# Attention block with group norm: one range test of the softmax sums per pair of heads, bias additions at the head of a burst, and a weight test that takes its minimum one chain later

## The chip, the cores and the metric

The kernel runs on one core of a Trainium2 chip. The metric is the device time of one execution in microseconds (us). Before the change the median of three timed runs was 1619.6 us (1618.7 to 1620.19). A separate execution was profiled; all durations below come from its trace.

## The reference

The input is `x` with 4 images of 512 channels and 48 x 48 = 2304 positions. Group norm (32 groups of 16 channels) is followed by a projection to queries, keys and values of 8 heads with 64 channels each, rounded to half precision; then softmax attention over the 2304 positions, an output projection in single precision, and the residual.

```python
hn = _group_norm(x, gn_scale, gn_bias)
qkv = jnp.einsum('oc,bchw->bohw', qkv_w, hn) + qkv_b[None, :, None, None]
qkv = qkv.reshape(b, 3, num_heads, d, t).astype(jnp.float16)
q, k, v = (qkv[:, 0], qkv[:, 1], qkv[:, 2])
scale = jnp.asarray(1.0 / math.sqrt(math.sqrt(d)), dtype=jnp.float16)
w = jnp.einsum('bhct,bhcs->bhts', q * scale, k * scale)
w = jax.nn.softmax(w, axis=-1)
a = jnp.einsum('bhts,bhcs->bhct', w, v).astype(jnp.float32)
out = jnp.einsum('oc,bchw->bohw', proj_w, a.reshape(b, c, hh, ww)) + proj_b[None, :, None, None]
return x + out
```

## The kernel before

**Two paths.** `fast_path` computes softmax without subtracting a maximum. While it runs it collects tests: every sum of exponentials must lie between `SUM_MIN` = 256 and `SUM_MAX` = 60000, and the split of the output weights into two parts must be exact. At the end the tests are added up into a flag; only where one failed does `general_path` compute everything again. With these inputs the fast path's result stands.

**Units of work.** Two heads are handled together, so there are 16 pairs `g` (4 per image `b`). For each pair the 2304 query positions are cut into five blocks `j`, four of 512 and one of 256 (`QBLOCKS`, `NQ` = 5). A block is worked off in bursts of three score tiles of 128 x 1024: `scores` issues the matmuls on TensorE (PE, L1084) and the exponentials on ScalarE (ACT, L1091); `add` sums the tiles on VectorE (DVE, L1140 and L1145); `values`, two bursts behind, multiplies with the values (PE, L1109). When a block ends, `avx` copies the product out of PSUM (DVE, L1118), `add_up` sums the accumulated exponentials over the partitions (PE, `sl`, L1168), `rows` copies the result (`slx`, L1184) and has the sync engine's queue (SP) send it as two small DMAs into a tile `sums` of 128 x 8. Then `check_sums` tests that tile on GpSimd (POOL, L1206 and L1207: twice a comparison and a product into `fine`), `invert` takes reciprocals, `spread` sends them back over a DRAM row into `ib`, and `divide` multiplies on POOL (`att`, L1233).

**Beside the bursts** stands a list `beside` of other PE work: the chains of the query and key projections for later pairs (`pqk`, L813, evacuated on DVE at L824), those of the values (`pv`, L865) and of the output projection of the image before (`pr`, L971). Each burst calls `fill(n)` once, which issues pieces of the list by a credit: the estimated work up to its due time over the bursts left. All chains beside the bursts share one PSUM bank (`ps_w`, one buffer), so a chain can start only when the one before has been evacuated by DVE; `av` and `sl` also share one bank (`ps_av`).

**The output weights** are loaded in four pieces (`wproj`, SP) and split during the first pair, a piece after each pair of `q` and `k` chains: on DVE the high part `whi` (L574), the remainder (L575) and its half precision form `wlo` (L578); on POOL the difference (L579) and its comparison with zero (L580); then on DVE the minimum over the comparison (L581, `tests<-wproj`).

**The output projection** of image `b - 1` runs during the next image, that of the last image in its own last pair and the tail. `att32` converts two of the four products of a block on POOL (`a`, L961) and two on ACT; `residual` loads `x` again (`r`, L916) and notes in `unbiased` that the bias must be added two bursts later. `add_bias` does so on POOL (L927); `proj_run` forces it for the rows it needs. DVE then adds the projection to `r` (L995), SP stores it.

**What sets the order.** The program is written by hand in the loop over bursts `n`: every engine works off its own queue in exactly this order, and waits on the others by semaphores. Within a burst the order is: loads due, `scores`, `rows` of a block that ended, `add`, (with an ended block) `fill`, `values`, `check_sums` and `invert`, `spread`, `divide`, (otherwise) `fill`, the joins, and then the biases that are due. `idle_once` puts a number of empty instructions into the queues of the first bursts.

Of the kernel before, what the change touches and what calls it, by code (L numbers as in the profile page):

```python
# [12 lines left out]
F32 = mybir.dt.float32  # L13
# [462 lines left out]
def fast_path(  # L476
# [93 lines left out]
        nc.sync.dma_start(wproj[c], proj_wT[bass.ts(c, P), :])  # L570

    def split_wproj(c):
        w = wproj.pop(c)
        nc.vector.tensor_scalar(whi[:, c, :], w, UP, None, ALU.mult)  # L574
        nc.vector.scalar_tensor_tensor(  # L575
            w, w, UP, whi[:, c, :].bitcast(F32), ALU.mult, ALU.subtract
        )
        nc.vector.tensor_copy(wlo[:, c, :], w)  # L578
        nc.gpsimd.tensor_tensor(w, w, wlo[:, c, :], ALU.subtract)  # L579
        nc.gpsimd.tensor_scalar(w, w, 0.0, None, ALU.is_equal)  # L580
        nc.vector.tensor_reduce(split_ok[:, c : c + 1], w, AX.X, ALU.min)  # L581

    mhalf = const.tile([P, 2], F32, name="mhalf")
    nc.gpsimd.memset(mhalf, -0.5)
# [15 lines left out]
            channel_multiplier=sign,  # L600
        )

    tests = const.tile([P, 2 * QB // P + NC], F32, name="tests")
    nc.gpsimd.memset(tests, 1.0)
    fine, split_ok = tests[:, : 2 * QB // P], tests[:, 2 * QB // P :]

# [439 lines left out]
    def expect_end(*engines):  # L1048

        taken = nc.values_load(  # L1050
            nothing[0:1, 0:1],
            engines=engines,
            min_val=0,
            max_val=1,
            skip_runtime_bounds_check_because="it is a constant",
        )
        tc.mark_branch_hint_location("fallback", taken, engines)
# [122 lines left out]
    def rows(g, j, sl):  # L1180

        o, n = QBLOCKS[j]
        sx = work.tile([P, QB], F32, tag="rows", name=f"slx_{g}_{j}")
        nc.vector.tensor_copy(sx[:, :n], sl[:, :n])  # L1184
        sm = small.tile([P, 2, QB // P], F32, tag="sums", name=f"sums_{g}_{j}")
        for h in range(2):
            nc.sync.dma_start(sm[:, h, : n // P], sx[h * D : h * D + 1, :n])
        sums[g, j] = sm
        return sx
# [7 lines left out]
        )  # L1197

    def check_sums(g, j):
        n = QBLOCKS[j][1]  # L1200
        sm = sums[g, j][:, :, : n // P]
        ok = fine.rearrange("p (h i) -> p h i", h=2)[:, :, : n // P]
        for op, limit in ((ALU.is_ge, SUM_MIN), (ALU.is_le, SUM_MAX)):
            t = small.tile([P, 2, QB // P], F32, tag="in", name=f"in_{g}_{j}")
            t = t[:, :, : n // P]
            nc.gpsimd.tensor_scalar(t, sm, limit, None, op)  # L1206
            nc.gpsimd.tensor_tensor(ok, ok, t, ALU.mult)  # L1207

    def invert(g, j):
        n = QBLOCKS[j][1]  # L1210
# [37 lines left out]
    def put_run(run, *args, when=None, after=0):  # L1248

        put([piece(0.05, lambda: run(*args), when=when)], after)  # L1250
# [41 lines left out]
    def put_qk(g, part, blocks=range(NQ)):  # L1292

        for j in blocks:
            put(qk_chain(g, part, j), (g - 2) * per_pair - 1, g)
# [39 lines left out]
    for b in range(B):  # L1335
        g = b * NPAIR
        old = b - 1
        if b == 0:
            for j in range(NQ):
                if j < NC:  # L1340
                    put_run(load_wproj, j)
                if j > 0:
                    put_run(split_wproj, j - 1)
                put_qk(g + 1, 1, (j,))
                put_qk(g + 1, 0, (j,))
            for block in SPARE:
                put_run(reload, *block)
# [183 lines left out]
    for n in range(end):  # L1531
        now[0] = n
        idle_once("sync", "scalar", "gpsimd")
        summed = block_at(n - BEHIND - 1)
        if not summed:
            load_due(n)
        wanted(stream[n][0])
        inside = n - BEHIND == soon[1]
        scores(stream[n], (lambda: values(stream[n - BEHIND])) if inside else None)
        if summed:  # L1540

            rows(*summed, add_up(*summed))
            load_due(n)
        if inside:
            expect_end(kinds.DVE)
        if n > 0:
            add(stream[n - 1])
        filled = summed or n - BEHIND - 1 in soon
        if filled:

            fill(n)
        if n >= BEHIND and not inside:
            values(stream[n - BEHIND])
        if block_at(n - BEHIND - 2):
            check_sums(*block_at(n - BEHIND - 2))
            invert(*block_at(n - BEHIND - 2))
        if block_at(n - BEHIND - 3):
            spread(*block_at(n - BEHIND - 3))
        if block_at(n - BEHIND - 4):

            divide(*block_at(n - BEHIND - 4))
        if not filled:
            fill(n)
        while joins:
            joins.popleft()()
        while unbiased and unbiased[0][0] <= n:
            add_bias()
        if n - BEHIND in soon:
            g, j = stream[n - BEHIND][:2]
            sx = rows(g, j, add_up(g, j))  # L1570
            if n - BEHIND == soon[1]:
                divide_here(g, j, sx, avx[g, j], nc.gpsimd)
        if n - BEHIND - 1 == soon[0]:
            check_sums(g, j)
            invert(g, j)
        if n - BEHIND - 2 == soon[0]:
            spread(g, j)
            divide(g, j)
# [143 lines left out]
```

## Time and profile before

| | |
|---|---|
| median of three runs | 1619.6 us |
| profiled execution: time, span | 1622.01 us, 1620.3 us |
| TensorE clock granted, mean | 0.994 |
| DVE busy | 1151.4 us (71%) |
| ACT busy | 1269.6 us (78%) |
| POOL busy | 453.4 us (28%), in 551 instructions |
| tests on POOL (L1206, L1207) | 100.2 and 62.9 us, 158 instructions each |
| bias additions on POOL (L927) | 108.2 us, 80 instructions |
| weight test on DVE (L581) | 2.7 us, 4 instructions |

The span runs from the first to the last instruction; the execution's own time is 1.7 us longer. Busy times are sums over one engine. In the views by stretches (windows) a row gives the busy time of every engine, the number of its instructions, and the mean of the clock that TensorE was granted; a stretch in which PE is busy less than its length is one in which PE waited. In the views of waits a row reads: engine, instruction and line, "<-" the engine and line that released it, then total us, number, longest. In timelines a row is start, duration, engine, line, operation, and in brackets the idle time before it with its releaser; instructions of one kind in succession are merged, so overlapping ends are normal.

### The profile page before, as it was taken

How to read it: one execution, taken by the hardware profiler on the slowest of the kernel's cores; microseconds unless marked ns; L12 is line 12 of the kernel's file. 1: busy time of each engine (PE TensorE's matmuls, PEld its weight loads, DVE VectorE, ACT ScalarE, POOL GpSimd, SP SyncE). 2: the span in 40 equal slices, each digit the busy share in tenths (PEclk: the TensorE clock that was granted, in tenths of full speed). 3: DMA queues.
4: the chain of work that ended last, by engine and by line, in shares of the span. 5: the costliest groups of instructions: out<-in, count | busy, mean ns of one | idle time of the engine just before them, and what ended most of it. 6: DMA issues, size and time to landing. Idle time of an engine off the chain costs nothing. (4 is left out here: it accounts for less than half of the span.)

```text
span 1620.3 us, 28874 instructions
## 1 busy us (share of the span) xinstructions
PE 1581.4 (98%) x11526; PEld 681.4 (42%) x11526; DVE 1151.4 (71%) x1302; ACT 1269.6 (78%) x1363; POOL 453.4 (28%) x551
## 2 busy tenths in 40 slices
PE   9988999999999999999999999999999999999997
PEld 3723444443333543445333354344533334434443
DVE  6256758876666678997666666899767676767776
ACT  4166777888888888888888888887878888888885
POOL 1021201222212122641112121274212121128744
PEclk9999999999999999999999999999999999999999
DMA  7001012000000014520000001352011000016423
GB/s 221 2 14 59 15 37 53 12 14 18 14 14 11 15 40 122 160 73 17 22 14 13 13 18 40 105 162 84 13 26 18 14 15 11 15 43 178 119 70 122
DMA packets 94900, 82.12 MB, mean 51 GB/s; under 512 B 50853, under 2 KB 60965, under 8 KB 94757
## 3 DMA queue, kind: packets, MB, share of 16 engines
q1 hardware_dynamic: 92724, 78.35, 17.6%
q8 instruction: 92, 1.51, 0.4%
q10 hardware_dynamic: 1904, 1.84, 0.4%
q14 instruction: 52, 0.42, 0.1%
q0 software_dynamic: 128, 0.01, 0.0%
HBM read 60.70 MB, written 19.17 MB: 49 GB/s over the span
## 5 line engine op out<-in xcount | busy, mean ns | idle before, releaser
L1091 ACT ACTIVATE p<-ps 128x1024 f16<-128x1024 f32 x1296 | 1233.2, 1025 | 319.9 <-PE ps L1084 315.5
L1140 DVE TENSOR_TENSOR acc<-acc,p 128x3072 f16<-128x3072 f16 x270 | 491.1, 1819 | 53.6 <-ACT p L1091 51.0
L813 PE MATMUL pqk<-x,wqkv 128*64 128x512 f32 (+1 forms) x2432 | 515.0, 553 | 4.7 <-DVE k L824 4.6
L1109 PE MATMUL av<-p,v 128*64 128x512 f16 (+1 forms) x2880 | 361.1, 364 | 0.0
L1084 PE MATMUL ps<-q,k 64*128 64x512 f16 (+1 forms) x2880 | 357.2, 359 | 0.5 <-DVE v L873 0.2
L1206 POOL TENSOR_SCALAR in<-sums 128x8 f32<-128x8 f32 (+1 forms) x158 | 100.2, 634 | 616.2 <-DMA sums<-slx 609.2
L865 PE MATMUL pv<-wqkv,x 128*64 128x256 f32 x2304 | 267.5, 379 | 0.2 <-DVE v L873 0.2
L813 PEld LDWEIGHTS pqk<-x,wqkv 128*64 128x64 f32 x2432 | 170.3, 138 | 212.4 <-issue 157.8
L1233 POOL TENSOR_TENSOR att<-avx,ib 128x512 f16<-128x512 f32 (+1 forms) x78 | 127.3, 1632 | 363.9 <-DMA ib<-row 332.0
L1084 PEld LDWEIGHTS <-k 64*128 64x128 f16 x2880 | 106.7, 94 | 288.4 <-issue 239.4
L1109 PEld LDWEIGHTS <-v 128*64 128x64 f16 x2880 | 131.5, 109 | 213.0 <-issue 168.6
L865 PEld LDWEIGHTS pv<-wqkv,x 128*64 128x64 f32 x2304 | 166.3, 137 | 81.2 <-DVE v L873 0.6
L1140 DVE TENSOR_TENSOR acc<-p,p 128x3072 f16<-128x3072 f16 x79 | 140.4, 1777 | 0.0
L1145 DVE TENSOR_TENSOR acc<-acc 128x1024 f16<-128x1024 f16 x156 | 114.6, 735 | 3.3
L824 DVE TENSOR_SCALAR q<-pqk,bqkv 128x512 f16<-128x512 f32 (+1 forms) x77 | 53.4, 694 | 81.2 <-PE pqk L813 80.8
L927 POOL TENSOR_TENSOR r<-r,bproj 128x512 f32<-128x512 f32 (+1 forms) x80 | 108.2, 1376 | 1.7 <-DMA r<-x_dram 1.7
L824 DVE TENSOR_SCALAR k<-pqk,bqkv 128x512 f16<-128x512 f32 (+1 forms) x75 | 52.1, 694 | 76.0 <-PE pqk L813 75.8
L873 DVE TENSOR_TENSOR v<-pv,bv 128x512 f16<-128x512 f32 x72 | 49.6, 689 | 78.0 <-PE pv L865 77.8
L971 PE MATMUL pr<-a,whi 128*128 128x512 f32 (+1 forms) x311 | 95.3, 422 | 2.1 <-POOL a L961 2.0
L1184 DVE COPY slx<-sl 128x512 f32<-128x512 f32 (+1 forms) x79 | 50.6, 640 | 62.1 <-PE sl L1168 61.9
L971 PE MATMUL pr<-att,wlo 128*128 128x512 f16 (+1 forms) x311 | 74.8, 360 | 12.5 <-DVE r L995 11.5
L995 DVE SCALAR_TENSOR_TENSOR r<-pr,r 128x512 f32<-128x512 f32 x75 | 51.4, 685 | 42.7 <-POOL r L927 27.5
(124 smaller groups left out, 547.3 us busy)
## 6 DMA issues: line engine op xcount, KB each, us to landing
r<-x_dram SPq DMA_DIRECT2D x72, 256.0 KB, 4.0
out_dram<-r SPq DMA_DIRECT2D x69, 256.0 KB, 2.3
ib<-row SPq DMA_DIRECT2D x126, 128.0 KB, 3.0
x<-x_dram SPq DMA_DIRECT2D x62, 256.0 KB, 4.0
x<-x_dram SPq DMA_DIRECT2D x16, 128.0 KB, 4.9
sums<-slx SPq DMA_DIRECT2D x128, 2.0 KB, 2.0
ib<-row SPq DMA_DIRECT2D x30, 64.0 KB, 3.3
wqkv<-qkv_wT_dram SPq DMA_DIRECT2D x2, 768.0 KB, 6.9
```

Of the source, the lines that this page charges most:

```text
L813: nc.tensor.matmul(pw[0][lo : lo + D, :n], wqkv[:, c, w0 + lo : w0 + lo + D], hn[b, c, j], start=(c == 0), stop=(c == NC - 1),)
L824: nc.vector.tensor_scalar(qk[g][part][:, o : o + n], pw[0][:, :n], bqkv[:, col : col + 1], SCALE, ALU.add, ALU.mult,)
L865: nc.tensor.matmul(pw[0][lo : lo + D, a, :], hn[b, c, i * P // QB][:, at + lo : at + lo + D], wqkv[:, c, 2 * C + half * C // 2 :][:, : C / ...
L927: nc.gpsimd.tensor_tensor(xt[:, i], xt[:, i], bias, ALU.add)
L971: nc.tensor.matmul(ps[:, :n], w[:, bass.ts(m, P)], a, start=(i == 0), stop=(i == len(steps) - 1),)
L1084: nc.tensor.matmul(ps[:, h, a * n : (a + 1) * n], kt[rows, bass.ts(i, P)], qt[rows, o : o + n], start=True, stop=True,)
L1091: nc.scalar.activation(pt[:, r], ps, AF.Exp)
L1109: nc.tensor.matmul(av[0][lo : lo + D, :n], vv[b, pr // 2][:, i, pr % 2 * P + lo : pr % 2 * P + lo + D], pt[:, r, h, a * n : (a + 1) * n], ...
L1140: nc.vector.tensor_tensor(t, before, pt, ALU.add)
L1145: nc.vector.tensor_tensor(t[:, 0], t[:, 0], t[:, r], ALU.add)
L1206: nc.gpsimd.tensor_scalar(t, sm, limit, None, op)
L1233: nc.gpsimd.tensor_tensor(atts[g][:, o : o + n], avx.pop((g, j))[:, :n], ibs.pop((g, j))[:, :n], ALU.mult,)
```

## The change

Three things are edited, all in `fast_path`.

1. The sums of a pair go into one of two fixed tiles of 128 x 40 (`sums_of`, by the pair's parity), five blocks of eight columns, filled once with `SUM_MIN` so that the four columns a short block leaves free pass. `check_sums` does nothing until a pair's last block and then tests all 40 columns with four instructions; in the last pair it tests 24 columns after its third block and 8 after its fourth. `tests` grows from 12 to 44 columns.
2. `add_bias` for the entries due is called before `add`, `fill`, `values`, `check_sums` and `divide` of a burst rather than after them.
3. The minimum over a split weight's test becomes a piece of its own, `test_split`, put behind the following `k` chain instead of directly behind the split.

```diff
     def split_wproj(c):
-        w = wproj.pop(c)
+        w = wproj[c]
...
         nc.gpsimd.tensor_scalar(w, w, 0.0, None, ALU.is_equal)
-        nc.vector.tensor_reduce(split_ok[:, c : c + 1], w, AX.X, ALU.min)
+
+    def test_split(c):
+        nc.vector.tensor_reduce(split_ok[:, c : c + 1], wproj.pop(c), AX.X, ALU.min)
...
-    tests = const.tile([P, 2 * QB // P + NC], F32, name="tests")
+    PER = 2 * QB // P
+    tests = const.tile([P, NQ * PER + NC], F32, name="tests")
     nc.gpsimd.memset(tests, 1.0)
-    fine, split_ok = tests[:, : 2 * QB // P], tests[:, 2 * QB // P :]
+    fine, split_ok = tests[:, : NQ * PER], tests[:, NQ * PER :]
+    sums_of = []
+    for s in range(2):
+        t = const.tile([P, NQ, 2, QB // P], F32, name=f"sums_{s}")
+        nc.gpsimd.memset(t, SUM_MIN)
+        sums_of.append(t)
...
-        sm = small.tile([P, 2, QB // P], F32, tag="sums", name=f"sums_{g}_{j}")
+        sm = sums_of[g % 2][:, j]
...
     def check_sums(g, j):
-        n = QBLOCKS[j][1]
-        sm = sums[g, j][:, :, : n // P]
-        ok = fine.rearrange("p (h i) -> p h i", h=2)[:, :, : n // P]
+
+        ends = (NQ - 1,) if g < NG - 1 else (NQ - 3, NQ - 2)
+        if j not in ends:
+            return
+        first = NQ - 2 if g == NG - 1 and j == NQ - 2 else 0
+        cols = slice(first * PER, (j + 1) * PER)
+        sm = sums_of[g % 2].rearrange("p j h i -> p (j h i)")[:, cols]
         for op, limit in ((ALU.is_ge, SUM_MIN), (ALU.is_le, SUM_MAX)):
-            t = small.tile([P, 2, QB // P], F32, tag="in", name=f"in_{g}_{j}")
-            t = t[:, :, : n // P]
+            t = small.tile([P, NQ * PER], F32, tag="in", name=f"in_{g}_{j}")[:, cols]
             nc.gpsimd.tensor_scalar(t, sm, limit, None, op)
-            nc.gpsimd.tensor_tensor(ok, ok, t, ALU.mult)
+            nc.gpsimd.tensor_tensor(fine[:, cols], fine[:, cols], t, ALU.mult)
...
                     put_run(split_wproj, j - 1)
                 put_qk(g + 1, 1, (j,))
+                if j > 0:
+                    put_run(test_split, j - 1)
                 put_qk(g + 1, 0, (j,))
...
         if inside:
             expect_end(kinds.DVE)
+        while unbiased and unbiased[0][0] <= n:
+            add_bias()
         if n > 0:
             add(stream[n - 1])
...
         while joins:
             joins.popleft()()
-        while unbiased and unbiased[0][0] <= n:
-            add_bias()
```

What this makes of the queues is shown at three places. The first is DVE's queue in the first pair, from the half precision form of the first weight piece (`wlo`) to the split of the second; `acc` are sums of exponentials, `k` and `q` evacuations of chains. Before:

```order
L578 CAST wlo<-wproj_692 128x512
L581 TENSOR_REDUCE tests<-wproj_692 128x1
L1140 TENSOR_TENSOR acc_0_746<-acc_0_746,p_0_2_733 128x3072
L1140 TENSOR_TENSOR acc_0_746<-acc_0_746,p_0_3_785 128x3072
L824 TENSOR_SCALAR k_695<-pqk_1_1_805,bqkv 128x512
L1140 TENSOR_TENSOR acc_0_746<-acc_0_746,p_0_4_817 128x3072
```

With the change:

```order
L578 CAST wlo<-wproj_696 128x512
L1148 TENSOR_TENSOR acc_0_750<-acc_0_750,p_0_2_737 128x3072
L1148 TENSOR_TENSOR acc_0_750<-acc_0_750,p_0_3_788 128x3072
L832 TENSOR_SCALAR k_699<-pqk_1_1_808,bqkv 128x512
L583 TENSOR_REDUCE tests<-wproj_696 128x1
L1148 TENSOR_TENSOR acc_0_750<-acc_0_750,p_0_4_820 128x3072
```

The minimum has moved behind two sums and the evacuation of `k`. The second place is POOL's queue during the output projection of the first image: `r_i_m` are the bias additions of block `i`, channels `m`; `a_0_2_2` and `a_0_2_3` the conversions of block 2; `att` the division of the running pair. Before:

```order
L927 TENSOR_TENSOR r_1_1_6498<-r_1_1_6498,bproj 128x512
L1206 TENSOR_SCALAR in_3_6676<-sums_3_6613 128x8
L1207 TENSOR_TENSOR tests<-tests,in_3_6676 128x8
L1206 TENSOR_SCALAR in_3_6679<-sums_3_6613 128x8
L1207 TENSOR_TENSOR tests<-tests,in_3_6679 128x8
L927 TENSOR_TENSOR r_1_2_6539<-r_1_2_6539,bproj 128x512
L927 TENSOR_TENSOR r_1_3_6617<-r_1_3_6617,bproj 128x512
L961 CAST a_0_2_2_6787<-att_2965 128x512
L961 CAST a_0_2_3_6789<-att_3938 128x512
L1233 TENSOR_TENSOR att_5746<-avx_3_6566,ib_3_6728 128x512
L927 TENSOR_TENSOR r_2_0_6647<-r_2_0_6647,bproj 128x512
```

With the change:

```order
L935 TENSOR_TENSOR r_1_1_6336<-r_1_1_6336,bproj 128x512
L935 TENSOR_TENSOR r_1_2_6377<-r_1_2_6377,bproj 128x512
L935 TENSOR_TENSOR r_1_3_6454<-r_1_3_6454,bproj 128x512
L935 TENSOR_TENSOR r_2_0_6484<-r_2_0_6484,bproj 128x512
L969 CAST a_0_2_2_6618<-att_2911 128x512
L969 CAST a_0_2_3_6620<-att_3850 128x512
L1244 TENSOR_TENSOR att_5605<-avx_3_6405,ib_3_6560 128x512
```

The four test instructions are gone, and the bias of `r_2_0` stands ahead of the two conversions and the division instead of behind them. The third place is the same queue in the last image. Before:

```order
L927 TENSOR_TENSOR r_2_0_15084<-r_2_0_15084,bproj 128x512
L1206 TENSOR_SCALAR in_2_15197<-sums_2_15145 128x8
L1207 TENSOR_TENSOR tests<-tests,in_2_15197 128x8
L1206 TENSOR_SCALAR in_2_15200<-sums_2_15145 128x8
L1207 TENSOR_TENSOR tests<-tests,in_2_15200 128x8
L927 TENSOR_TENSOR r_1_3_15090<-r_1_3_15090,bproj 128x512
L927 TENSOR_TENSOR r_2_1_15123<-r_2_1_15123,bproj 128x512
L961 CAST a_2_2_2_15261<-att_10643 128x512
L961 CAST a_2_2_3_15263<-att_11793 128x512
L927 TENSOR_TENSOR r_2_0_15149<-r_2_0_15149,bproj 128x512
L927 TENSOR_TENSOR r_2_2_15163<-r_2_2_15163,bproj 128x512
```

With the change:

```order
L935 TENSOR_TENSOR r_2_0_14670<-r_2_0_14670,bproj 128x512
L935 TENSOR_TENSOR r_1_3_14674<-r_1_3_14674,bproj 128x512
L935 TENSOR_TENSOR r_2_1_14709<-r_2_1_14709,bproj 128x512
L935 TENSOR_TENSOR r_2_0_14732<-r_2_0_14732,bproj 128x512
L935 TENSOR_TENSOR r_2_2_14748<-r_2_2_14748,bproj 128x512
L969 CAST a_2_2_2_14840<-att_10357 128x512
L969 CAST a_2_2_3_14842<-att_11478 128x512
```

Here the tests are gone too, and two biases now stand ahead of the conversions that PE needs.

## The prediction

> **What bounds the kernel now.** I read the page's busy times first, then stretches of the span, to see where the busiest engine waits.
>
> ```profile
> span 1620.3 us, 28874 instructions
> PE 1581.4 (98%) x11526; PEld 681.4 (42%) x11526; DVE 1151.4 (71%) x1302; ACT 1269.6 (78%) x1363; POOL 453.4 (28%) x551
> ```
>
> PE is busy all but 38.9 us. Work taken off POOL or DVE can shorten the span only where PE waits for it, or where waiting slows PE's clock. The stretches show where that is:
>
> ```profile
> 84.00:140.00 56.00, 45.88 (x260) 15.50 (x260) 35.51 (x43) 34.26 (x36) 13.31 (x13) 0.93 0.04 10
> 140.00:640.00 500.00, 499.90 (x3754) 206.09 (x3752) 357.55 (x394) 402.28 (x424) 101.45 (x133) 1.00 0.12 32
> 640.00:720.00 80.00, 77.00 (x536) 37.22 (x532) 73.52 (x96) 64.65 (x73) 48.42 (x49) 0.98 0.45 131
> ...
> 1040.00:1130.00 90.00, 85.93 (x590) 40.31 (x588) 81.43 (x104) 73.33 (x84) 55.23 (x55) 1.00 0.45 131
> ...
> 1460.00:1600.00 140.00, 132.35 (x860) 62.49 (x858) 103.73 (x104) 119.42 (x136) 95.98 (x93) 1.00 0.42 124
> ```
>
> Behind the length stand the busy times of PE, PE's weight loads, DVE, ACT and POOL, then the granted clock. PE waits 10.1 us from 84 to 140 (the split of the output weights), and 3.0, 4.1 and 7.65 us in the three output projections, 14.7 together; in the 500 us behind the split it waits 0.1. The rest is the start and the tail. The list of waits names the causes:
>
> ```profile
> POOL in L1206 <- DMA sums<-slx: 609.2, 59, 15.3
> ...
> DVE r L995 <- POOL r L927: 27.5, 18, 3.2
> ...
> PE pr L971 <- DVE r L995: 11.5, 13, 2.2
> DVE tests L581 <- POOL wproj L580: 11.4, 4, 2.9
> ...
> PE sl L1168 <- DVE avx L1118: 5.5, 2, 3.1
> PE pqk L813 <- DVE k L824: 4.6, 3, 2.2
> ```
>
> The last two rows, 5.5 + 4.6 = 10.1 us, are the whole of PE's idle time at the split. The 11.5 us are most of that in the projections.
>
> **The weight test (edit 3).** One of the four pieces in the timeline, and a later row of undisturbed matmuls:
>
> ```profile
> 85.87 0.43 DVE L578 CAST wlo<-wproj 128x512 f16<-128x512 f32 x1
> 86.38 1.16 POOL L579 TENSOR_TENSOR wproj<-wproj,wlo 128x512 f32<-128x512 f32 x1 [59.23 <-DVE wlo L578]
> ...
> 88.57 1.88 PE L813 MATMUL pqk<-x,wqkv 128*64 128x512 f32 x8
> ...
> 89.18 0.69 DVE L581 TENSOR_REDUCE tests<-wproj 128x1 f32<-128x512 f32 x1 [2.88 <-POOL wproj L580]
> ...
> 89.78 3.61 DVE L1140 TENSOR_TENSOR acc<-acc,p 128x3072 f16<-128x3072 f16 x2
> ...
> 93.31 0.75 DVE L824 TENSOR_SCALAR k<-pqk,bqkv 128x512 f16<-128x512 f32 x1
> ...
> 94.11 5.38 PE L813 MATMUL pqk<-x,wqkv 128*64 128x512 f32 x16 [2.14 <-DVE k L824]
> ...
> 116.98 3.60 PE L813 MATMUL pqk<-x,wqkv 128*64 128x512 f32 x16
> ```
>
> DVE's minimum stands in its queue right behind `wlo` and waits 2.88 us for two POOL instructions, of which the first is shown. Queued behind it are two sums and the evacuation of `k`, and for that PE waits 2.14 us. Then 16 matmuls take 5.38 us instead of 3.60. The clock, in stretches of 1 us some two us after each of the four waits, says why (it is the last number but two):
>
> ```profile
> 95.00:96.00 1.00, 1.00 (x6) 0.50 0.00 0
> ...
> 110.00:111.00 1.00, 1.00 (x6) 1.00 0.00 0
> ...
> 126.00:127.00 1.00, 1.00 (x4) 0.50 0.00 0
> ...
> 140.00:141.00 1.00, 1.00 (x8) 0.50 0.11 18
> ```
>
> After three of the four, PE ran at half clock. By the matmul rows one such spell costs 5.38 - 3.60 = 1.8 us; I take 1.7, so 5.1 for three. (The stretch from 84 to 140 agrees: 7% of 56 us is 3.9, and the last spell reaches beyond it.)
>
> With the change the minimum comes behind the next evacuation of `k`. I place the queue by these rows: `wlo` ends at 86.30, the two sums take 3.61 and end at 89.9, `k`'s chain ends on PE at 90.45, so `k` is out by 91.2, ahead of 91.97 (94.11 - 2.14), when PE wants the bank. POOL has ended by 89.18, before the minimum is reached. So DVE doesn't wait, and PE doesn't. In the second and third piece one sum of 1.8 us and the end of `k`'s chain stand between. In the fourth it is only a join, `avx` and a short `k`: DVE may still wait there, by less than today's 2.9 us, with `slx` queued behind it, for whose bank `av` waits; I leave 0.2 us of PE waiting. The instruction itself stays (0.69 us). Gain: 10.1 + 5.1 - 0.2 = **15.0 us**. Bound: 9.9 if the half clock has another cause; nothing below that, since nothing comes in front of the evacuations.
>
> By the Trainium skill, "TensorE: Matmul & The Clock Gate", section "What's actually happening", PE falls to half clock after an idle window of about 3.4 us. By that rule gaps of 2 to 3 us would not do it, and the sum would be 9.9. The trace's 0.50 behind a gap of 2.14 us speaks against it here.
>
> **The tests (edit 1).** Of 316 test instructions 68 stay: 15 pairs with four, the last with eight.
>
> ```profile
> L1206 POOL TENSOR_SCALAR in<-sums x158: 232/243/1837, 113.1 to 1606.8; 128x8 f32<-128x8 f32 x128, 128x4 f32<-128x4 f32 x30
> ```
>
> A comparison over 8 columns takes 0.24 us where nothing disturbs it (least, median and longest stand before the times). 40 columns the trace doesn't show: at least the same, at most the longest, 1.84; I take 0.3, near the median. POOL loses most of its test work, but outside the projections it waits 609 us for those very sums, so there it is worth nothing. SP's transfers, `invert` and `divide` keep their places, and the tail keeps its four instructions over 8 columns.
>
> **The bias additions (edits 1 and 2).** In the first projection:
>
> ```profile
> 676.92 0.69 DVE L995 SCALAR_TENSOR_TENSOR r<-pr,r 128x512 f32<-128x512 f32 x1 [1.47 <-POOL r L927]
> ```
>
> ```profile
> 687.06 1.02 PE L971 MATMUL pr<-att,wlo 128*128 128x512 f16 x4 [2.17 <-DVE r L995]
> 687.74 1.79 PE L971 MATMUL pr<-a,whi 128*128 128x512 f32 x4
> ...
> 692.70 1.28 PE L971 MATMUL pr<-a,whi 128*128 128x512 f32 x4
> ```
>
> DVE waited 1.47 us for the bias `r_2_0`, which stood behind two conversions and a division, and worked without a pause from there to PE's wait of 2.17 us. A half clock spell followed (1.79 us against 1.28); I take 1.7 for it, as above. Now the bias stands in front: PE's wait shrinks to 0.7, too short for a spell. Gain 1.5 + 1.7 = 3.2. In the second projection DVE likewise lost 0.93 us to a bias:
>
> ```profile
> 1085.58 0.69 DVE L995 SCALAR_TENSOR_TENSOR r<-pr,r 128x512 f32<-128x512 f32 x1 [0.93 <-POOL r L927]
> ```
>
> It had no pause from there until PE's next wait: gain 0.9. In the last image POOL is itself the slow one:
>
> ```profile
> 1490.17 1.64 POOL L1206 TENSOR_SCALAR in<-sums 128x8 f32<-128x8 f32 x1
> ...
> 1492.64 2.04 POOL L927 TENSOR_TENSOR r<-r,bproj 128x512 f32<-128x512 f32 x2
> ...
> 1571.53 1.28 POOL L1233 TENSOR_TENSOR att<-avx,ib 128x512 f16<-128x512 f32 x1 [2.27 <-DMA ib<-row]
> ```
>
> ```profile
> 1494.46 1.02 PE L971 MATMUL pr<-att,wlo 128*128 128x512 f16 x4 [0.54 <-DVE r L995]
> 1496.82 1.06 PE L971 MATMUL pr<-a,whi 128*128 128x512 f32 x2 [0.86 <-POOL a L961]
> ...
> 1513.95 0.49 PE L971 MATMUL pr<-a,whi 128*128 128x512 f32 x1 [0.53 <-POOL a L961]
> ...
> 1574.58 1.02 PE L971 MATMUL pr<-att,wlo 128*128 128x512 f16 x4 [1.07 <-DVE r L995]
> ...
> 1596.43 0.38 PE L971 MATMUL pr<-att,wlo 128*128 128x512 f16 x1 [0.42 <-DVE r L995]
> ```
>
> The tests from 1490.17 to 1492.64 hold it 2.5 us; they go. But two biases (1.0 us each in the row behind them) move ahead of the conversions that follow. PE's four waits from there to 1514 (the first two and the last are shown) add up to 3.4 us; I take 2.5 of them as gone. At 1571 biases stand behind a division that waits 2.27 us for its transfer; they now stand before it, and I take the waits of 1.07 and 0.42 us as gone: 1.5. Sum of the projections: 3.2 + 0.9 + 2.5 + 1.5 = **8 us**, bounded by 0 and by all waits there with the spell, 14.7 + 1.7 = 16.4; a loss is the last rival's case. The planner counts four pieces of 0.05 us more, which moves half chains by a burst in a few places; PE has the same instructions, and I take that as nothing, within 2 us either way.
>
> **Sum.** 15 + 8 = 23 us. The profiled execution took 1622.0, so 1599.0 for its like; the median lies 2.4 below it: 1619.6 - 23 = 1596.6, **1597 us**.
>
> **Rivals.**
> - Only the weight test pays. The projections' waits stay, because DVE's other work sets them (it is busy 73.5 of 80 us in the first): 1619.6 - 15 = 1605. Against it: 27.5 us of DVE's waits there are for biases. Chance 0.24.
> - The half clock spells have another cause than these gaps and stay (the skill's rule): 1619.6 - 9.9 - 6.3 = 1603. Chance 0.05.
> - All of it goes: 1619.6 - 15.2 - 16.4 = 1588. Against it: DVE's 73.5 of 80 us again. Chance 0.08.
> - The change doesn't reach PE: another wait takes over the 10 us at the split, for instance one for ACT. Against it: ACT is busy 34 of 56 us there. About 1619.6. Chance 0.03.
> - Slower: in the last image biases now stand ahead of five pairs of conversions. If each pair comes two biases later at the slowest that this row shows (2.65 us) and PE waits for all of it, 5 x 5.3 = 26.5 us come on top: 1619.6 - 15 + 26.5 = 1631. It decides from a delay of 3 us per pair. Against it: the tests give POOL back as much. Chance 0.06.
>
> ```profile
> L927 POOL TENSOR_TENSOR r<-r,bproj x80: 607/1041/2651, 644.5 to 1594.6; 128x512 f32<-128x512 f32 x64, 128x256 f32<-128x256 f32 x16
> ```
>
> **How the numbers follow.** The forecast has 0.54. The range 1590 to 1609 takes in the forecast, the first two rivals and the 2 us of moved chains; outside are all of it gone, no change, and slower, 0.17 together. About 0.2% (3.2 us) is what a measurement can tell from no change: faster by more has 0.91, within it 0.03, slower 0.06.
>
> **What would show it.** Right: no wait of DVE for POOL's comparison, PE busy over 55 of the 56 us from 84 at clock 1.00, the rows `sl` and `pqk` gone from PE's waits, and PE's wait for `r` down from 11.5 to about 4 us. Wrong: half clock without a gap ahead of it, new waits of PE for POOL's `a` in the last image, or waits at the moved chains between 140 and 640 us.

## The result, and the profile after

The changed kernel takes **1604.1 us** (median of 6, 1603.0 to 1605.3) where the kernel before, timed beside it, takes 1619.4 (median of 6): a ratio of 0.9906, 95% interval 0.9893 to 0.9918. That is 15.3 us less. The forecast was 23 less, 1597, with a range of 1590 to 1609. The time lies in the range, 7 us above the forecast, and the rival "only the weight test pays", 1605, lies nearest.

The head of the changed kernel's page (span, then busy time of the engines):

```profile
span 1602.0 us, 28595 instructions
...
PE 1575.6 (98%) x11526; PEld 679.2 (42%) x11526; DVE 1156.8 (72%) x1302; ACT 1269.6 (79%) x1363; POOL 344.5 (22%) x305
```

POOL lost 109 us of work (453.4 before). PE waits 26.4 us instead of 38.9, and is itself 5.8 us shorter busy with the same 11526 matmuls: about 5 us of that is the clock, for windows of 1 us show four half-clock spells of some 1.7 us each in the profile before and one in this one (ahead of the kernel's last 10 us). The stages of the changed kernel, about 14 to 18 us earlier than before (length, then the busy times of PE, PE's loads, DVE, ACT and POOL, then the granted clock):

```profile
84.00:126.00 42.00, 41.75 (x266) 14.72 (x264) 35.22 (x40) 33.36 (x36) 17.89 (x9) 1.00 0.06 14
126.00:626.00 500.00, 498.96 (x3754) 205.47 (x3752) 361.75 (x396) 404.24 (x426) 58.95 (x53) 1.00 0.12 32
626.00:706.00 80.00, 76.19 (x528) 36.88 (x524) 72.94 (x95) 63.75 (x72) 39.02 (x35) 0.98 0.45 131
...
1024.00:1114.00 90.00, 86.83 (x596) 40.30 (x592) 82.29 (x106) 75.02 (x85) 43.38 (x37) 1.00 0.44 131
...
1443.00:1582.00 139.00, 134.83 (x876) 63.18 (x878) 108.06 (x107) 121.46 (x138) 85.81 (x73) 1.00 0.42 125
```

The split of the weights is clean: 0.25 us of waiting in 42 us, at clock 1.00 (10.1 us in 56 at 0.93 before). The projections are not: PE waits 3.8 us in the first (3.0 before), 3.2 in the second (4.1), 4.2 in the last image (7.65), and the clock of the first is 0.98 as it was. The list of waits of the changed kernel (total, times, longest):

```profile
POOL att L1244 <- DMA ib<-row: 949.9, 65, 21.7
...
DVE r L1003 <- POOL r L935: 10.5, 8, 3.2
...
PE pr L979 <- DVE r L1003: 8.5, 9, 2.7
...
DVE tests L583 <- POOL wproj L580: 3.2, 3, 1.6
...
PE pr L979 <- POOL a L969: 1.8, 3, 0.7
```

The row to look at is the pair in the middle. DVE waits 17 us less for biases than before (27.5 to 10.5), and PE gets 3 us of it (11.5 to 8.5). POOL's 610 us of waiting for the sums became waiting for the rows that it divides by: there was never anything to win there, as forecast.

### The profile page after: what moved, and what is told of

The parts are those of the page before. It is cut to its first block, busy times and chain, and to the rows that moved or that the text cites. A ratio compares the mean times of both kernels' runs of the same rounds, so it can differ in the third digit from the quotient of the medians.

```text
span 1602.0 us, 28595 instructions
## 1 busy us (share of the span) xinstructions
PE 1575.6 (98%) x11526; PEld 679.2 (42%) x11526; DVE 1156.8 (72%) x1302; ACT 1269.6 (79%) x1363; POOL 344.5 (22%) x305
## 5 line engine op out<-in xcount | busy, mean ns | idle before, releaser
L1244 POOL TENSOR_TENSOR att<-avx,ib 128x512 f16<-128x512 f32 (+1 forms) x78 | 132.3, 1696 | 1050.0 <-DMA ib<-row 949.9
L1153 DVE TENSOR_TENSOR acc<-acc 128x1024 f16<-128x1024 f16 x156 | 120.1, 770 | 3.3
L1003 DVE SCALAR_TENSOR_TENSOR r<-pr,r 128x512 f32<-128x512 f32 x75 | 51.4, 685 | 36.8 <-PE pr L979 13.9
L1126 DVE COPY avx<-av 128x512 f32<-128x512 f32 (+1 forms) x79 | 50.5, 639 | 35.7 <-PE av L1117 35.7
```

The costliest lines, as they stand in the source:

```text
L1003: nc.vector.scalar_tensor_tensor(xt, ps, DOWN, xt, ALU.mult, ALU.add)
L1153: nc.vector.tensor_tensor(t[:, 0], t[:, 0], t[:, r], ALU.add)
L1244: nc.gpsimd.tensor_tensor(atts[g][:, o : o + n], avx.pop((g, j))[:, :n], ibs.pop((g, j))[:, :n], ALU.mult,)
```

## The experiments

Twelve experiments ran. The ratio of each is to the kernel before on the same chip; the table stands here and is read in what follows. "Idle" is PE's idle time in the profiled execution, summed over all waits of 0.15 us and more that the timeline shows: at the split, in the first and the second projection, and in the last image.

| kernel | median us | ratio, 95% interval | split | 1st | 2nd | last |
|---|---|---|---|---|---|---|
| before (its first profile) | 1619.4 | | 10.1 | 2.9 | 3.8 | 7.4 |
| e1 before, again | 1620.3 | 1.0005, 0.9996 to 1.0014 | 10.1 | 3.1 | 3.2 | 7.3 |
| e2 edit 3 alone | 1606.9 | 0.9920, 0.9906 to 0.9933 | 1.2 | 3.5 | 3.6 | 7.2 |
| e3 edit 1 alone | 1620.6 | 1.0009, 1.0000 to 1.0018 | 10.4 | 4.3 | 3.6 | 6.4 |
| e4 edit 2 alone | 1619.6 | 0.9998, 0.9989 to 1.0007 | 10.1 | 3.4 | 2.9 | 5.7 |
| changed (first profile) | 1604.1 | 0.9906, 0.9893 to 0.9918 | 1.2 | 3.7 | 2.9 | 4.0 |
| e5 changed, again | 1603.1 | 0.9900, 0.9879 to 0.9921 | 1.2 | 4.3 | 3.5 | 4.1 |
| e6 edits 1 and 3 | 1606.1 | 0.9918, 0.9898 to 0.9939 | 1.2 | 3.9 | 3.6 | 6.5 |
| e7 edits 2 and 3 | 1604.6 | 0.9904, 0.9883 to 0.9925 | 1.2 | 3.6 | 3.8 | 4.6 |
| e8 no biases | 1590.0 | 0.9820, 0.9799 to 0.9840 | 1.2 | 0.0 | 0.4 | 0.6 |
| e9 biases aside | 1599.6 | 0.9869, 0.9853 to 0.9886 | 1.2 | 3.5 | 2.8 | 3.7 |
| e10 norm in steps | 1601.7 | 0.9884, 0.9868 to 0.9901 | 1.1 | 2.4 | 3.3 | 3.9 |
| e11 biases on ACT | 1607.1 | 0.9915, 0.9899 to 0.9932 | 1.1 | 1.8 | 2.2 | 8.7 |
| e12 biases shared | 1598.9 | 0.9877, 0.9860 to 0.9893 | 1.2 | 0.8 | 1.3 | 3.2 |

### Which edit pays: e1 to e7

e1 is the kernel before with nothing edited.

> The kernel before, unchanged, profiled and timed a second time. Theory A (the profiled execution on which the forecast's sum was made is typical; the 2.4 us between it and the median are spread evenly): PE idle 38.9 us again within 1 us, three half-clock spells at the split of the weights and one in the first projection. Theory B (part of the missing gain stood only in that one execution): PE idle or the count of spells is lower, and the span of the profile is near 1617.5 us. Time: no change, ratio 1.000 within 0.002.

Its profile has a span of 1615.7, 4.6 us under the first one, with nearly the same waits (28.7 us against 30.3 in sum). What differs is the clock. The timeline of its PE shows the two waits behind which the prediction had counted half-clock spells, and its windows of 1 us the clock behind them:

```profile
93.77 3.69 PE L813 MATMUL pqk<-x,wqkv 128*64 128x512 f32 x16 [2.13 <-DVE k L824]
...
684.88 1.02 PE L971 MATMUL pr<-att,wlo 128*128 128x512 f16 x4 [2.17 <-DVE r L995]
```

```profile
95.00:96.00 1.00, 1.00 (x7) 0.39 (x5) 0.38 (x1) 0.00 (x0) 0.00 (x0) 1.00 0.00 0
...
687.00:688.00 1.00, 1.00 (x12) 0.34 (x8) 1.00 (x3) 1.00 (x2) 1.00 (x2) 1.00 0.43 156
```

The same waits, to 0.01 us, and the clock stays at 1.00; 16 matmuls take 3.69 us where they took 5.38. Of the four spells two are there, at the second half of the split. Theory B holds: part of the forecast's gain was a matter of that one execution. The timed runs agree. Over 58 executions of the kernel before that were timed beside the experiments, e1's among them, the median time is 1622.1 us at a mean granted clock of 0.993 (6 runs; one more at 0.992), 1620.3 at 0.994 (25), 1618.9 at 0.995 (18) and 1617.3 at 0.996 (8): a step of 0.001 costs about 1.5 us, near the 1.7 of one spell.

e2 has only the minimum moved:

```diff
-        nc.vector.tensor_reduce(split_ok[:, c : c + 1], w, AX.X, ALU.min)
+    def test_split(c):
+        nc.vector.tensor_reduce(split_ok[:, c : c + 1], wproj.pop(c), AX.X, ALU.min)
...
                 put_qk(g + 1, 1, (j,))
+                if j > 0:
+                    put_run(test_split, j - 1)
                 put_qk(g + 1, 0, (j,))
```

> Only the minimum over the weights' test is moved behind the next chain (edit 3). The forecast's sum says 15.0 us off, 1604.4 us, PE idle near 0.2 us at the split, no half clock there. If the half clock there has another cause than the gaps: 9.9 us off, 1609.5. If the whole measured gain of 15.3 us is this edit (the projections pay nothing): 1604, and waits for r in the projections stay near 11.5 us. If the projections gave their share and this edit gave less: 1607 to 1611.

12.8 us come off. The split's idle goes from 10.1 to 1.2, no spell is left there, the projections keep 14.3 us. So this edit carries most of the 15.3, and the spells did hang on those waits. Its last part is a new wait, which the changed kernel has as well. From that kernel's timeline, the first piece and the fourth:

```profile
86.19 2.60 POOL L579 TENSOR_TENSOR wproj<-wproj,wlo 128x512 f32<-128x512 f32 x1 [59.22 <-DVE wlo L578]
...
88.89 2.90 POOL L580 TENSOR_SCALAR wproj<-wproj 128x512 f32<-128x512 f32 x1
...
91.81 0.69 DVE L583 TENSOR_REDUCE tests<-wproj 128x1 f32<-128x512 f32 x1 [0.74 <-POOL wproj L580]
...
126.39 0.69 DVE L583 TENSOR_REDUCE tests<-wproj 128x1 f32<-128x512 f32 x1 [1.63 <-POOL wproj L580]
127.00 0.68 DVE L1192 COPY slx<-sl 128x512 f32<-128x512 f32 x1
...
127.73 0.84 PE L1117 MATMUL av<-p,v 128*64 128x512 f16 x6 [0.94 <-DVE slx L1192]
```

POOL's two instructions took 1.16 and 1.5 us while DVE stood and waited for them. Now DVE's sums run beside them, and they take 2.60 and 2.90. So DVE still reaches the minimum before POOL is done, and in the fourth piece `slx` and PE wait for it.

e3 has only the range test once per pair, e4 only the biases at the burst's head:

```diff
+        ends = (NQ - 1,) if g < NG - 1 else (NQ - 3, NQ - 2)
+        if j not in ends:
+            return
```

> Only the range test once per pair of heads over 40 columns (edit 1); biases and the weights' test as before. The forecast put no own price on it, but its 2.5 us in the last image (tests that hold POOL from 1490 to 1492) hang on it: 1617 us. If POOL's time is worth nothing to PE: 1619.4, no change. If a 40 column test in the first projection delays the norm's power on POOL: 1619.4 to 1621.

```diff
+        while unbiased and unbiased[0][0] <= n:
+            add_bias()
         if n > 0:
             add(stream[n - 1])
...
-        while unbiased and unbiased[0][0] <= n:
-            add_bias()
```

> Only the bias additions at the burst's head (edit 2). The forecast's sum hangs 3.2 + 0.9 + 1.5 us on it: 1613.8 us, and PE's wait of 2.2 us in the first projection down to 0.7. Theory B (DVE catches up from the bias wait before PE needs it, and PE's wait there is set by the chain of the norm, which has a power on POOL that now stands behind a bias): that wait stays at 2.2 to 2.7 us with its half-clock spell, and the whole is worth 0 to 2 us: 1617.5 to 1619.4. Slower, if conversions in the last image come too late behind biases: above 1622.

Neither moves the time by what can be measured. e3: the idle time in the last image falls by 0.8 to 1.0, and in the first projection it grows by more. e4: 12.0 us idle in the projections against 14.1 and 13.5 in the two profiles of before, so about 2 us were won there; but the wait of 2.2 us in the first projection, of which the forecast took 1.5 us and a spell away, became 2.4. The 2 us don't show in the time. The mean granted clock of its 11 runs is 0.9935 against 0.9944 beside it, which at 1.5 us a step would be 1.4 of them; that is an argument, not a test.

e5 is the changed kernel again, e6 has the biases back at the end of the burst, e7 the test back at every block.

> The changed kernel, unchanged, a second time, beside the next three. All theories: 1603 to 1605 us where before has 1619.5. It is the mark for them; whether a half-clock spell follows the wait of 2.7 us in the first projection is open (two profiles of before had the same wait of 2.17 us there, one with and one without a spell).

> The changed kernel with the bias additions back at the burst's end (edits 1 and 3). If the two edits add nothing each (as alone): the same as the weight test alone, 1606.9. If the bias edit carries the 2.8 us between that kernel and the changed one: 1606 to 1607. If the pair check carries them: 1604. The forecast's sum would put 5.6 us on the bias edit: 1610.

> The changed kernel with the range test back at every block, 8 columns (edits 2 and 3). If the bias edit carries the 2.8 us: 1604. If the pair check carries them: 1606 to 1607. If they come only from both together (POOL has to be free of tests for the biases at the head to cost nothing): 1606 to 1607 here and in the run before as well.

By the medians of the runs timed together with e5 the bias edit is worth 3.0 us (1606.1 to 1603.1) and the pair check 1.5 (1604.6 to 1603.1); each interval is some 3 us wide to either side, so only the order of size is shown. The idle sums say the same: 14.0 us in e6, 12.1 in e7, 11.9 and 10.6 in the two profiles of the changed kernel. Together the two edits bring 2 to 4 us on top of edit 3 (by the two ratios of the changed kernel 2.3 and 3.2), not 8. And the first projection's wait stands in all of them, between 2.2 and 2.7 us.

### Why the projections keep their waits: e8 to e11

e8 leaves the output bias out: the additions are gone, the loads of the residual stay.

```diff
-        for i, m in enumerate(chunks):
-            bias = bproj[:, m : m + 1].to_broadcast((P, xt.shape[2]))
-            nc.gpsimd.tensor_tensor(xt[:, i], xt[:, i], bias, ALU.add)
```

> The changed kernel without the additions of the output bias (they are left out, the loads of the residual stay). It is the most that any place of the biases can give. The forecast's step (DVE's lateness in the first projection comes from a bias): the wait of 2.7 us there falls under 1 us, and the projections' PE idle from 10.6 to about 6. Theory B (the norm's chain sets it): that wait stays above 1.5 us; the waits of 0.9 and 1.4 us in the second projection, where two normalizations took 2.4 us instead of 1.0 beside biases, go. Time 1597 to 1601.

Both theories fall short: 13 to 14 us go, more than either allowed, and 1.0 us of idle time is left in the projections together. So the biases are the cause, also of the wait that theory B puts down to the norm, and DVE's instructions stand in the same order. They take less time, though: the 1302 instructions of DVE are busy 1156.8 and 1159.8 us in the two profiles of the changed kernel, and 14 to 17 us less in e8:

```profile
PE 1572.5 (99%) x11526; PEld 678.4 (43%) x11526; DVE 1142.5 (72%) x1302; ACT 1268.9 (80%) x1363; POOL 230.9 (15%) x225
```

The rows of one burst tell how. First the changed kernel's timeline, three of DVE's evacuations of `r` and what stands between the last two, with POOL's instructions beside it:

```profile
662.84 0.69 DVE L1003 SCALAR_TENSOR_TENSOR r<-pr,r 128x512 f32<-128x512 f32 x1 [0.64 <-PE pr L979]
...
666.32 0.69 DVE L1003 SCALAR_TENSOR_TENSOR r<-pr,r 128x512 f32<-128x512 f32 x1
666.48 1.04 POOL L935 TENSOR_TENSOR r<-r,bproj 128x512 f32<-128x512 f32 x1
666.93 2.20 DVE L1148 TENSOR_TENSOR acc<-acc,p 128x3072 f16<-128x3072 f16 x1
667.48 2.24 POOL L666 TENSOR_TENSOR rstd<-veps,mhalf 128x2 f32<-128x2 f32 x1
...
669.68 1.03 POOL L935 TENSOR_TENSOR r<-r,bproj 128x512 f32<-128x512 f32 x1
669.75 1.01 DVE L676 COPY both<-rstd 128x32 f32<-128x32 f32 x1 [0.62 <-POOL rstd L666]
...
671.36 1.03 POOL L935 TENSOR_TENSOR r<-r,bproj 128x512 f32<-128x512 f32 x1
671.45 0.97 DVE L687 TENSOR_TENSOR mga<-cols,ga 128x4 f32<-128x4 f32 x1
...
673.11 0.68 DVE L1003 SCALAR_TENSOR_TENSOR r<-pr,r 128x512 f32<-128x512 f32 x1
...
673.85 1.86 PE L979 MATMUL pr<-att,wlo 128*128 128x512 f16 x4 [2.68 <-DVE r L1003]
```

The same burst in the timeline of e8:

```profile
664.72 0.69 DVE L1000 SCALAR_TENSOR_TENSOR r<-pr,r 128x512 f32<-128x512 f32 x1
664.77 0.72 POOL L666 TENSOR_TENSOR rstd<-veps,mhalf 128x2 f32<-128x2 f32 x1 [0.61 <-DVE both L669]
...
665.32 1.75 DVE L1145 TENSOR_TENSOR acc<-acc,p 128x3072 f16<-128x3072 f16 x1
...
666.99 0.17 DVE L676 COPY both<-rstd 128x32 f32<-128x32 f32 x1
...
667.68 0.16 DVE L687 TENSOR_TENSOR mga<-cols,ga 128x4 f32<-128x4 f32 x1
...
668.53 0.68 DVE L1000 SCALAR_TENSOR_TENSOR r<-pr,r 128x512 f32<-128x512 f32 x1
```

Between the last two `r` it is 6.8 us with biases and 3.8 without: the sum takes 2.20 instead of 1.75, the copy 1.01 instead of 0.17, a product of four columns 0.97 instead of 0.16, and DVE stands 0.62 for the power on POOL (`rstd`). That power begins 1.16 us after the first of these two `r` instead of 0.05, because an addition stands ahead of it in POOL's own queue, and then takes 2.24 us beside a sum of DVE instead of 0.72. Each long DVE instruction begins within 0.1 us of a POOL instruction's start or runs beside one, and the small ones end with it (669.75 + 1.01 against 669.68 + 1.03). None of them reads what the biases are added to. The Trainium skill, "SBUF — State Buffer", section "Who interferes with whom", has a rule for this: DVE and GpSimd share a pair of access ports, and where instructions of both need it, the one issued first keeps it to its end while the other stands still. By that section DVE needs it when it reads two inputs from SBUF, as in the sum and the product, and a copy can need it in its faster modes; other instructions with at most one input from SBUF don't. The trace agrees for the copy and the product here, in the other direction for the power, and for the evacuations of `r`, which read PSUM and one tile of SBUF and keep their 0.69 us beside an addition (666.32).

e9 takes only the dependence away. POOL's 80 additions stay at their places, but work on a scratch tile that nobody reads, so the residual gets no bias.

```diff
+    aside = const.tile([P, 416], F16, name="aside")
+    nc.gpsimd.memset(aside, 0.0)
...
-            nc.gpsimd.tensor_tensor(xt[:, i], xt[:, i], bias, ALU.add)
+            nc.gpsimd.tensor_tensor(aside[:, :n], aside[:, :n], bias, ALU.add)
```

> The changed kernel with POOL's 80 bias additions kept at their places, but done on a scratch tile of 416 f16 columns that nobody reads (so the residual gets no bias, and DVE waits for none). Arrival theory (what PE lost was DVE waiting for a bias to be ready): as without biases, near 1590 us, PE's waits in the projections gone. Shared access theory (a POOL instruction and DVE's sums hold each other up while they run, whoever needs the result): PE's waits in the two first projections stay mostly, 4 to 7 us of the 7, time 1598 to 1603 us.

The list of waits of e9:

```profile
DVE r L1006 <- PE pr L982: 31.0, 35, 2.6
...
PE pr L982 <- DVE r L1006: 7.6, 10, 2.2
```

DVE waits for no bias any more; where it waited 10.5 us for them it now waits for PE itself (31.0 against 13.9). PE still waits 9.9 us in the projections, with 2.15 at the same place. DVE is as slow as in the changed kernel, 1159.4 us busy. Of the 10 to 11 us that go when the additions go, then, the larger part, about 9, is what they do while they run, to DVE and to the power behind them in POOL's queue; at most 2 us is that `r` comes late. At the wait of the first projection no run parts the stretched instructions of DVE from the power that comes late. The time is lower than the changed kernel's by some 4 us (5 to 6 by the ratios), and the part of that beyond the waits stays open; the scratch additions also differ a little from the real ones (0.87 us instead of 1.04 at this place, 102 us instead of 105 in all).

e10 deals the norm out over more bursts, and puts the weights' minimum behind both chains (the new function `apart`, with the norm's small products, isn't shown):

```diff
...
-                tasks.append((n, 0.9, lambda: coefficients(b)))
+                tasks.append((n, 1.2, lambda: coefficients(b)))
+                tasks.append((n, 1.2, lambda: apart(b)))
...
                 put_qk(g + 1, 1, (j,))
+                put_qk(g + 1, 0, (j,))
                 if j > 0:
                     put_run(test_split, j - 1)
-                put_qk(g + 1, 0, (j,))
```

> The changed kernel with the norm's coefficients dealt out over two bursts (copy and transpose in one, the three small products in the next, normalizations after them), and the weights' minimum behind both chains instead of one. If the chain of the norm in one burst sets the wait of 2.7 us in the first projection: it falls below 1 us there, and the waits after it grow by less than 1. If only the sum of DVE's work counts: the 2.7 us turn up spread over the next two or three waits. At the split of the weights the wait of 0.94 us should go in any case. Time 1599 to 1603 us by the first, 1602 to 1603 by the second.

PE in the timeline of e10, at the place of the 2.7 us:

```profile
672.75 1.02 PE L983 MATMUL pr<-att,wlo 128*128 128x512 f16 x4 [0.48 <-DVE r L1007]
...
676.47 1.02 PE L983 MATMUL pr<-att,wlo 128*128 128x512 f16 x4 [0.24 <-DVE r L1007]
...
680.18 1.02 PE L983 MATMUL pr<-att,wlo 128*128 128x512 f16 x4 [0.68 <-DVE r L1007]
```

2.7 us became 0.5, and the three together 1.4. So the norm's chain matters too: that wait needs both, the chain in one burst and the biases that stretch it, and goes when either goes. At the split the expectation failed. 0.94 us went, but 0.59 and 0.24 came: the minimum now stands in front of the next piece's work, with `avx` and PE's `sl` behind it.

e11 has the biases on ACT, and the weights' minimum behind both chains as in e10:

```diff
...
-            nc.gpsimd.tensor_tensor(xt[:, i], xt[:, i], bias, ALU.add)
+            by_scalar(xt[:, i], 1.0, bproj[:, m : m + 1])
...
```

> The changed kernel with the bias additions on ACT instead of POOL (same places in the program; the result is whole), and the weights' minimum behind both chains. Shared access theory: DVE's instructions run at their short times (1.75 us a sum, 0.55 a normalization), PE's waits for r fall from 8.5 us to under 3, and the time is near 1592 to 1596 us, unless ACT, busy 64 of 80 us in the first projection, comes late with exponentials: then PE waits for ACT by several us and the time is 1600 to 1610. Arrival theory: little change, since a bias on ACT stands behind three exponentials: 1600 to 1605.

Its list of waits:

```profile
PE ps L1091 <- ACT p L1098: 11.2, 26, 0.5
...
PE pr L978 <- DVE r L1002: 1.2, 2, 1.0
```

The waits for `r` fall from 8.5 to 1.2 us and DVE's busy time to 1142.1 us, as the shared access asks for: here the biases are still added and DVE still needs them. And ACT becomes late with its exponentials, 11.2 us in 26 waits of at most 0.5, most of them in the last image (8.7 us idle there). The gain is there and is more than paid back at another engine: 1607.1 us.

### A faster version: e12

In the first two projections alone, the biases of all blocks but the first go to ACT, and all conversions to POOL; the last image stays as in the changed kernel.

```diff
+            if key[0] < B - 1 and key[1] > 0:
+                by_scalar(xt[:, i], 1.0, bproj[:, m : m + 1])
+                continue
...
-            if beside or c in beside_exps() and not (pairs == LAST and left_over(b, j)):
+            mine = b < B - 1 or c in beside_exps()
+            if beside or mine and not (pairs == LAST and left_over(b, j)):
```

> The changed kernel with, in the first two projections alone, the biases of all blocks but the first on ACT and in exchange all conversions of the attention on POOL; the last image stays as changed. The result is whole. Shared access theory: PE's waits for r in the first two projections fall from 7 us to under 3 without ACT coming late, no half-clock spell there, the last image's waits stay at 4 us: 1597 to 1600 us. If POOL's conversions hold DVE up as the biases did, or come late themselves: PE waits for POOL's a, and the time stays at 1602 to 1605. If ACT comes late again: PE waits for p by 2 us or more there, 1602 to 1606.

1598.9 us, ratio 0.9877 (0.9860 to 0.9893): some 4 to 5 us under the changed kernel (0.9906 and 0.9900 in its two measurements) and 21 under the kernel before. Its list of waits:

```profile
PE pr L983 <- DVE r L1007: 2.5, 3, 1.6
...
PE pr L983 <- POOL a L973: 2.3, 6, 0.5
```

The first two projections have 2.2 us of idle time left of 6.6 to 7.8, and its profile shows no half-clock spell ahead of the kernel's end. The two kernels weren't timed side by side and their intervals touch, so the size is rough; but all four runs of e12 (1596.9 to 1599.9) lie under all ten of the changed kernel (1602.5 to 1605.3).

## Why the prediction was right in direction and its time 7 us too low

**What bounds the kernel.** Right: PE, and only where it waits. 109 us of POOL's work went and the time followed PE's waits and clock alone.

**The weight test, 15.0 us forecast.** Right mechanism, 12.8 measured (e2). Two sizes in it were off. "So DVE doesn't wait, and PE doesn't" and the 0.2 us left for the fourth piece: DVE waits 3.2 us in three of the four, and PE 0.94, because POOL's two instructions were priced as the row showed them with DVE standing still, and DVE now works beside them. And the three spells of 1.7 us were taken as certain; the second profile of before has two, and over all runs before stands at a mean clock of 0.9944 and e2 at 0.9972, two to three spells apart. The rival that the spells have another cause fell: in none of the profiles with edit 3 is there a spell at the split.

**The tests.** The pair check is worth nothing alone and 1.5 us beside the others, inside the noise. The sum gave it 2.5 us of the last image together with the biases. The instruction over 40 columns, estimated at 0.3 us, has a median of 0.31 and a longest of 1.75 us.

**The bias additions, first projection: 3.2 us forecast, nothing gained.** This is the step that failed. It read that DVE waited 1.47 us for the bias and "worked without a pause from there to PE's wait of 2.17 us", and concluded that PE's wait shrinks by nearly the 1.47. The reading is right, the conclusion isn't. Without that wait DVE stands 0.64 us for PE's `pr` instead (the row at 662.84), so only some 0.8 us were to be had. And these are lost again on the way: from that evacuation to the one that PE waits for it is 10.3 us in the changed kernel (662.84 to 673.11) and 9.4 in the kernel before (676.92 to 686.33). A bias that moves ahead doesn't stop stretching DVE's instructions, it stretches others; and it can come ahead of the norm's power as well. PE's wait is 2.2 (e7), 2.4 (e4) and 2.7 us (changed), against 2.2 with the biases at the burst's end. The half-clock spell that the forecast took away came in e4 and in one of the changed kernel's two profiles. Rows of the kernel before told it: there the sum and the power run at their short times, and a product of four columns takes 0.96 us beside an addition, with the same end:

```profile
680.74 0.73 POOL L658 TENSOR_TENSOR rstd<-veps,mhalf 128x2 f32<-128x2 f32 x1
...
681.28 1.75 DVE L1140 TENSOR_TENSOR acc<-acc,p 128x3072 f16<-128x3072 f16 x1
...
684.58 1.03 POOL L927 TENSOR_TENSOR r<-r,bproj 128x512 f32<-128x512 f32 x1
684.67 0.96 DVE L679 TENSOR_TENSOR mga<-cols,ga 128x4 f32<-128x4 f32 x1
...
686.33 0.68 DVE L995 SCALAR_TENSOR_TENSOR r<-pr,r 128x512 f32<-128x512 f32 x1
```

**Second projection, 0.9 us forecast.** 3.8 to 2.9 in the first pair of profiles, but 3.2 and 3.5 in the second pair: not settled, and small. Its last two waits, 0.9 and 1.4 us, stand wherever POOL adds the biases (0.6 and 1.2 in e9), and go in e8, e11 and e12.

**Last image, 4.0 us forecast.** 3.4 and 3.2 us less idle time in the two profiles: nearly right, with some luck in the parts. The four waits of 3.4 us, of which 2.5 were to go, became three of 1.5. Of the two at the division the one of 1.07 us went and the one of 0.42 stayed; in its place went one of 0.45 that the sum hadn't named. There POOL is late itself, and both edits relieve it (7.2 without either, 6.5 with the pair check, 4.6 with the bias edit, 4.1 with both).

**Sum.** 12.8 instead of 15.0, and 2.5 instead of 8: 15.3. "Only the weight test pays", at 1605, named the right reason for the first two projections ("DVE's other work sets them"), without the cause of DVE's slowness. The slower rival, conversions late behind biases, didn't come: PE's waits for POOL's `a` went from 2.0 to 1.8 us. That is the pair check's doing. Without it PE's wait of 0.86 us for `a` at 1496.82 grows, in e4 and then in e7:

```profile
1496.95 1.06 PE L971 MATMUL pr<-a,whi 128*128 128x512 f32 x2 [1.63 <-POOL a L961]
```

```profile
1482.18 1.06 PE L973 MATMUL pr<-a,whi 128*128 128x512 f32 x2 [1.61 <-POOL a L963]
```

So the tests give POOL the time back that the biases ahead of the conversions cost, as the prediction argued against this rival; the pair check is of use beside the bias edit, and alone it moved nothing.

## What to carry to other kernels

A wait that is removed upstream is worth only what is left of it at the next point where someone waits for the engine: look what else would have held the engine up there, and whether the work in between takes as long as before. On two engines that hold each other up, moving an instruction moves the delay along with it; take it to a third engine, and only as much of it as that engine's bursts have room for. Price an instruction from rows in which its neighbours work as they will after the change, and a clock spell from several executions, not one.

## What the runs showed of the hardware

The half clock is not a fixed price of a wait. Waits of 2.13 and 2.14 us at the same instruction were followed by a spell of 1.7 us in three profiles of kernels with the old split and by none in one; behind the wait of the first projection (2.2 to 2.7 us) a spell came in five profiles of ten. Two profiles of the changed kernel, first and second (e5), in windows of 1 us just behind that wait of 2.68 and 2.67 us (the granted clock is the last number but two):

```profile
674.00:675.00 1.00, 1.00 (x3) 0.29 (x2) 1.00 (x1) 0.00 (x0) 0.00 (x0) 0.50 0.28 106
```

```profile
674.00:675.00 1.00, 1.00 (x5) 0.62 (x5) 1.00 (x1) 0.00 (x0) 0.00 (x0) 1.00 0.17 66
```

The wait of 2.38 us at the split's second piece had no spell in any of the four profiles with the old split, and the one of 3.1 us had it in all four; in e7 one followed the wait of 1.61 us shown above. The Trainium skill, "TensorE: Matmul & The Clock Gate", section "What's actually happening", has the gate judge activity in windows of about 3.4 us that run free of the kernel. That a same wait meets a spell in one execution and not in the next agrees with free windows; that waits of 2.1 us and less can suffice does not agree with an idle window of 3.4 us as the condition. The spells go with most of the spread of the kernel before, 1617 to 1622 us: its times step with the mean clock.
